# A graph layer on one core: bins ordered by branch, norms and input sums as queued VectorE steps, fillers between bin groups, first norms ahead of small loads

## The chip, the cores and the metric

The kernel runs on one core of a Trainium2 chip. TensorE (PE in the profile) multiplies matrices, VectorE (DVE) and ScalarE (ACT) work element by element, GpSimd (POOL) does a few small steps and issues some DMAs, SyncE (SP) issues most DMAs. Each engine works through its own list of instructions in order; semaphores join the lists. The metric is the device time of one execution in microseconds.

## The reference

64 graphs of 256 nodes with 256 features. All of it is float32.

```python
h = relu(layernorm(x))
# convolution branch: 1x1, then 17 taps along the nodes
c = relu(bn1(conv1(h)))
x_conv = relu(bn2(conv2(c)) + h)
# message branch
s = h @ w_se.T + b_se                       # 3 columns
A = exp(-|s_n - s_m|^2) * adj
x_nmp = A @ relu(h @ w_msg.T + b_msg)
# GRU gates
gi = [x_conv, x_nmp] @ w_ih.T + b_ih;  gh = h @ w_hh.T + b_hh
r = sigmoid(gi_r + gh_r); z = sigmoid(gi_z + gh_z)
n = tanh(gi_n + r * gh_n)
out = x + (1 - z) * n + z * h
```

## The kernel before

Graphs go in tiles of two (`G = 2`), so there are 32 tiles `i`; four tiles (`PB`) make a block `b`, and there are eight blocks. The convolution of 17 taps is done as a transform of length 16 along the nodes: products of the transformed input with the transformed filter in 16 bins, two bins at a time, so eight calls `products(b, 0)` to `products(b, 7)`, called P0 to P7 in the prediction. Bins 0 to 7 (P0 to P3) are the odd bins, the others the even bins. Each call uses three of five PSUM buffers "acc"; ScalarE copies one, VectorE subtracts and adds (lines 639, 640) into `Yv` (odd) or `Yu` (even, the same memory as V). There are three other PSUM buffers, "aux", for all else.

The forward transform is made by `fft.odd` (on V, with the sums in `Sv`) and `fft.even` (on U, with `PT`), the inverse by `odd_back`, `q_back`, `p_back` and `join`; `residual` then applies bn2 and a relu and gives the gates their operand `Yv`. T is scratch for all of these.

Before the first block a prologue makes the transformed filters: 57 calls of `filters` (one or two matmuls of 256 columns of `points` with `taps`, a copy by ScalarE into one of six buffers `fo`, a store to DRAM on SyncE's queue). They are read back bin by bin as `wb` (three buffers, SyncE's queue). In the prologue also run, for each of the first four tiles, `transpose_h` (transposes on TensorE, relu on ScalarE into `hT`, and the load of the x of two tiles later), `norm` of the next tile, `conv1`, and `split` (line 560: sums and differences of conv1's output `h1` into V and U).

In a block, tiles i to i+3 get their messages and gates while the next four tiles get norm, transposes, conv1 and split. `embed` makes s on TensorE and four small ScalarE steps (lines 664 to 667) on a single pair of tiles `ld`, `rd`; `message` a matmul, an add of the bias on VectorE (line 680) and a relu; `affinity` the exponent on ScalarE and the product with adj on VectorE (line 695); `transpose_a` and `aggregate` follow. `gates` needs twelve matmul passes with `Yv` (rows `acc<-Yv,w_ih`) after the rest.

The order of TensorE's work is written out by hand in the loop over blocks. The order on VectorE comes from a planner, `Pace`: it adds up the assumed time of TensorE and VectorE; steps of the transforms wait in one queue, and as many of them are put ahead of a direct VectorE instruction as fit before its operand is due. `flush(mark)` empties the queue up to a mark. Norm and split are direct instructions before the change. HW DMAs of SyncE and ScalarE use eight semaphores in turn, and an issue waits for the DMA that had its semaphore before.

Of the kernel before, what the change touches and what calls it, by code (L numbers as in the profile page):

```python
# [41 lines left out]
class Fft:  # L42
# [97 lines left out]

    def odd_back(self, Y, T):
# [5 lines left out]
        for h, t in ((0, T16), (2, T5)):  # L147
            q += [self.stt(Y(1, h, 2), T(1, h, 2), t, T(0, h, 2)),
                  self.stt(Y(1, h + 4, 2), T(0, h, 2), -t, T(1, h, 2))]
        even, odd = (lambda c, s: Y(c, s, 2, 2)), (lambda c, s: Y(c, s + 1, 2, 2))  # L150

        q += [self.sub(T(0, 0, 4), Y(0, 0, 4, 2), Y(0, 1, 4, 2)),
              self.sub(T(1, 0, 2), even(1, 0), odd(1, 4)),
              self.add(T(1, 2, 2), even(1, 4), odd(1, 0)),
              self.add(Y(0, 0, 4, 2), Y(0, 0, 4, 2), Y(0, 1, 4, 2)),
              self.add(even(1, 0), even(1, 0), odd(1, 4)),
              self.sub(even(1, 4), even(1, 4), odd(1, 0))]
        for h in (0, 2):
            q += [self.stt(Y(None, h + 1), T(None, 2 + h // 2), T8, T(None, h // 2)),
                  self.stt(Y(None, h + 5), T(None, h // 2), -T8, T(None, 2 + h // 2))]  # L160
# [106 lines left out]
ROOTS = [cmath.exp(1j * math.pi * (f + 16 * c) / 16) for c in (0, 1) for f in (1, 9, 5, 13)]  # L267
# [25 lines left out]
def kernel(  # L293
# [75 lines left out]
    def load_x(i):  # L369
        X[i] = work.tile([P, G * MC, D], FP, name="x", bufs=2)  # L370
        load_rows(X[i], x, i, nc.sync)

    def load_adj(i):
        ADJ[i] = work.tile([P, G * MC, N], FP, name="adj")
        load_rows(ADJ[i], adj, i, nc.gpsimd)
# [20 lines left out]
    def vec(src, name):  # L396
        k = src.shape[0] // P
        t = const.tile([P, k], FP, name=name)
        nc.sync.dma_start(out=t, in_=src.rearrange("(k p) -> p k", p=P))
        return t  # L400

    def fold_bn(params, name, factor=1.0):
        g, b, m, v = (vec(a, f"{name}_{s}") for a, s in zip(params, "gbmv"))
# [10 lines left out]


# [10 lines left out]
    w_c1 = const.tile([P, DC, D], FP)  # L426
    nc.scalar.dma_start(out=w_c1, in_=c1_wT.rearrange("(k p) o -> p k o", p=P))
    s1, h1_shift = fold_bn(bn1, "bn1")
# [15 lines left out]
    w_se = const.tile([P, DC, KD], FP)  # L444
    nc.gpsimd.memset(w_se, 0.0)
    for r in (0, 32, 64):
        nc.gpsimd.dma_start(out=w_se[:, :, r:r + SE], in_=se_wT.rearrange("(k p) s -> p k s", p=P))
    b_se = const.tile([P, 1], FP)
    for r in (0, 32, 64):
        nc.gpsimd.dma_start(out=b_se[r:r + SE, :], in_=se_b.rearrange("(s o) -> s o", o=1))  # L450
    w_msg = const.tile([P, DC, D], FP)
    nc.sync.dma_start(out=w_msg, in_=msg_wT.rearrange("(k p) o -> p k o", p=P))
    b_msg = const.tile([P, D], FP)
    nc.gpsimd.dma_start(out=b_msg, in_=bass.AP(tensor=msg_b.tensor, offset=msg_b.offset, ap=[[0, P], [1, D]]))
    load_adj(0)

    w_ih = const.tile([P, 2 * DC, 3 * D], FP)
    w_hh = const.tile([P, DC, 3 * D], FP)
    s2, h2_shift = fold_bn(bn2, "bn2", 1.0 / L)
    b_ih, b_hh = vec(ih_b, "b_ih"), vec(hh_b, "b_hh")  # L460
    b_rz = const.tile([P, 2 * DC], FP)
    nc.vector.tensor_add(b_rz, b_ih[:, :2 * DC], b_hh[:, :2 * DC])
    nc.vector.tensor_scalar(b_rz, b_rz, 0.5, None, ALU.mult)
    b_se2 = const.tile([P, 1], FP)
    nc.vector.tensor_scalar(b_se2[0:SE, :], b_se[0:SE, :], 2.0, None, ALU.mult)

# [21 lines left out]
    pace = Pace()  # L488

    def mm(p, w, v, columns, **kw):  # L490
        nc.tensor.matmul(p, w, v, **kw)  # L491
        pace.tensor(columns)

    def transpose(p, v):
        nc.tensor.transpose(p, v, ident)  # L495
        pace.tensor(P / 2)

    PSUM, ACT = 0.2, 0.9

    HT, MSG, E, AT, XNM = {}, {}, {}, {}, {}  # L500


    def norm(i):
        if i >= B // G:
            return
        st = work.tile([P, G * MC, 6], FP, name="st")
        mv = work.tile([P, G * MC, 2], FP, name="mv")
        for j in range(G * MC):
            pace.vector(D)
            nc.vector.bn_stats(st[:, j, :], X[i][:, j, :])  # L510
        for j in range(G * MC):
            pace.vector(1)
            nc.vector.bn_aggr(mv[:, j, :], st[:, j, :])
        rstd = work.tile([P, G * MC], FP, name="rstd")
        pace.vector(1)
        nc.vector.tensor_scalar(rstd, mv[:, :, 1], LN_EPS, None, ALU.add)
        nc.gpsimd.tensor_tensor(rstd, rstd, neg_half, ALU.pow)
        pace.vector(0, pace.dve + 1.4)
# [418 lines left out]
```

## Time and profile before

| | us |
|---|---|
| runs (three) | 2120.24, 2119.30, 2120.24; median 2120.24 |
| profiled execution, its own time | 2119.11 |
| its span | 2117.3 |
| TensorE busy | 1944.6 (92%) |
| VectorE busy | 1396.6 (66%) |
| ScalarE busy | 648.0 (31%) |
| GpSimd busy | 162.8 (8%) |
| first P0 begins | 143.01 |
| granted TensorE clock, mean | 0.977 |

A row of the timeline gives start, duration, engine, line, operation, tiles (out<-in), shape, how many followed each other, and in brackets the idle time of the engine before and what ended it. TensorE does each float32 matmul in two passes, so its counts are twice those of the program; durations of its groups include the end of the last pass, so starts are subtracted rather than ends. PEld is its weight load, SPq and ACTq are DMA issues on the queues of SyncE and ScalarE. In a list of waits the three numbers are the total, the count and the longest.

### The profile page before, as it was taken

The page shows a single profiled execution, that of the slowest core. Times are in us where ns is not written, and L with a number is a line of the kernel's source. Part 1 is how long each engine was busy: PE and PEld are TensorE (multiplying, and loading weights), DVE is VectorE, ACT ScalarE, POOL GpSimd, SP SyncE. Part 2 cuts the span into 40 slices and gives each one's busy share as a digit, 9 for nine tenths or more (in the row PEclk, how much of TensorE's full clock was granted, in tenths as well). Part 3 has the DMA queues.
Part 4 walks back from the last instruction along what each step waited for, and adds up shares of the span by engine and source line. Part 5 has one row for each costly group of instructions (what it writes and reads, how often), then busy time and mean ns, then how long its engine had stood idle before and what let it go on. Part 6 is the DMA issues. An engine that isn't in the chain of part 4 may idle for free.

```text
span 2117.3 us, 21204 instructions
## 1 busy us (share of the span) xinstructions
PE 1944.6 (92%) x7966; PEld 1221.2 (58%) x7966; DVE 1396.6 (66%) x2580; ACT 648.0 (31%) x1050; POOL 162.8 (8%) x246
## 2 busy tenths in 40 slices
PE   0889899998999899998999989998999989999897
PEld 0669445774449544694456844586455944568453
DVE  1379846796387845968367873879549784688532
ACT  0543422243313432224322432224322243223221
POOL 2000010100000001000001001000010100100000
PEclk9999999999999999999999999999999999999999
DMA  4766011540116202170124501163021711135010
GB/s 130 245 186 201 20 31 54 159 140 10 50 55 200 80 20 75 50 229 20 40 55 128 163 18 40 55 189 100 17 67 34 230 46 35 40 99 153 8 34 26
DMA packets 94164, 187.12 MB, mean 88 GB/s; under 512 B 23118, under 2 KB 40014, under 8 KB 94062
## 3 DMA queue, kind: packets, MB, share of 16 engines
q1 hardware_dynamic: 63368, 132.58, 20.1%
q0 software_dynamic: 27888, 50.58, 9.0%
q10 hardware_dynamic: 2806, 2.61, 0.4%
q8 instruction: 62, 1.02, 0.2%
q14 instruction: 40, 0.33, 0.0%
HBM read 156.55 MB, written 29.10 MB: 88 GB/s over the span
## 4 chain that ended last, share of the span: by engine, by line
PE 76%; DVE 13%; DMA 5%; ACT 3%; issue 2%; SPq 1%; POOL 1%; ACTq 0%; POOLq 0%; DVEq 0%
PE acc L491 58%; PE aux L491 15%; PE aux L495 3%; DMA wb<-filt 3%; DVE V L61 2%; DVE Yv L64 1%; DVE T L64 1%; DVE Yv L656 1%; DVE V L64 1%; DVE T L61 1%; DVE V L58 1%; DMA taps<-in_c_wT_dram 1%; DVE e L695 1%; SPq L442 1%; ACT Yv L657 1%
## 5 line engine op out<-in xcount | busy, mean ns | idle before, releaser
L491 PE MATMUL acc<-Yv,w_ih 128*128 128x512 f32 x768 | 359.1, 619 | 46.8 <-ACT Yv L657 46.8
L491 PE MATMUL acc<-hT,w_hh 128*128 128x512 f32 x768 | 350.6, 592 | 0.0
L491 PE MATMUL acc<-xnm,w_ih 128*128 128x512 f32 x768 | 350.4, 592 | 0.0
L491 PEld LDWEIGHTS acc<-Yv,w_ih 128*128 128x128 f32 x768 | 152.2, 199 | 244.7 <-issue 187.1
L491 PEld LDWEIGHTS acc<-xnm,w_ih 128*128 128x128 f32 x768 | 145.9, 190 | 183.7 <-issue 183.7
L491 PEld LDWEIGHTS acc<-hT,w_hh 128*128 128x128 f32 x768 | 144.1, 190 | 161.6 <-issue 156.7
L744 ACT ACTIVATE tr<-acc,b_rz 128x512 f32<-128x512 f32 x64 | 44.0, 687 | 553.7 <-PE acc L491 553.7
L746 DVE SCALAR_TENSOR_TENSOR gn<-tr,gn 128x512 f32<-128x512 f32 x64 | 44.2, 691 | 210.5 <-ACT tr L744 210.5
L560 DVE TENSOR_TENSOR V<-h 128x512 f32<-128x512 f32 x64 | 44.0, 688 | 157.7 <-ACT h L546 157.7
L491 PE MATMUL aux<-w_msg,hT 128*128 128x256 f32 x512 | 116.5, 380 | 12.9 <-ACT rd L667 12.9
L491 PE MATMUL acc<-V,wb 128*128 128x128 f32 x1024 | 126.1, 277 | 0.0
L491 PE MATMUL aux<-aT,msg 128*128 128x256 f32 x512 | 124.8, 400 | 0.6 <-ACT aT L706 0.6
L491 PEld LDWEIGHTS acc<-U,wb 128*128 128x128 f32 x1024 | 120.0, 192 | 5.1 <-issue 2.5
L491 PE MATMUL acc<-U,wb 128*128 128x128 f32 x1024 | 122.1, 275 | 0.0
L491 PEld LDWEIGHTS acc<-V,wb 128*128 128x128 f32 x1024 | 121.0, 194 | 0.0
L58 DVE SCALAR_TENSOR_TENSOR V<-T,V 128x256 f32<-128x256 f32 (+2 forms) x224 | 120.0, 609 | 0.3
L491 PE MATMUL acc<-hT,w_c 128*128 128x512 f32 x256 | 117.3, 601 | 1.1 <-ACT hT L533 1.1
L491 PEld LDWEIGHTS aux<-w_msg,hT 128*128 128x128 f32 x512 | 96.1, 190 | 35.2 <-ACT rd L667 14.6
L491 PEld LDWEIGHTS aux<-aT,msg 128*128 128x128 f32 x512 | 101.2, 202 | 19.3 <-issue 3.8
L495 PE MATMUL aux<-ident,x 128*128 128x128 f32 x256 | 37.1, 285 | 72.8 <-DVE x L521 51.6
L491 PE MATMUL acc<-Sv,wb 128*128 128x128 f32 x512 | 70.2, 281 | 21.5 <-DMA wb<-filt 13.9
L772 POOL DMA_DIRECT2D out_dram<-y x64 | 39.1, 615 | 642.3 <-DVE y L771 618.8
(124 smaller groups left out, 2662.8 us busy)
## 6 DMA issues: line engine op xcount, KB each, us to landing
wb<-filt SPq DMA_DIRECT2D x120, 768.0 KB
x<-in_x_dram SPq DMA_DIRECT2D x64, 256.0 KB
adj<-in_adj_dram POOLq DMA_DIRECT2D x64, 256.0 KB, 5.7
y<-in_x_dram POOLq DMA_DIRECT2D x64, 256.0 KB, 4.2
out_dram<-y POOLq DMA_DIRECT2D x64, 256.0 KB, 5.1
filt<-fo SPq DMA_DIRECT2D x36, 252.0 KB
wb<-filt SPq DMA_DIRECT2D x8, 512.0 KB
filt<-fo SPq DMA_DIRECT2D x18, 154.0 KB
```

What stands on the lines that cost most here:

```text
L58: return self.step(out, lambda: self.v.scalar_tensor_tensor(out, x, s, y, op0=ALU.mult, op1=ALU.add))
L61: return self.step(out, lambda: self.v.tensor_add(out, x, y))
L64: return self.step(out, lambda: self.v.tensor_sub(out, x, y))
L442: nc.sync.dma_start(out=taps[dc * REST * TAPS:(dc + 1) * REST * TAPS, DC * NG, :], in_=c2_wT[dc * P + NG * KG:(dc + 1) * P].rearrange("k t ...
L491: nc.tensor.matmul(p, w, v, **kw)
L495: nc.tensor.transpose(p, v, ident)
L560: nc.vector.tensor_sub(V(None, s, 4)[:, A], a, bb)
L656: nc.vector.scalar_tensor_tensor(v, v, s2[:, o:o + 1], HT[i][:, o, :], op0=ALU.mult, op1=ALU.add)
L657: nc.scalar.activation(v, v, AF.Relu, bias=h2_shift[:, o:o + 1])
L744: nc.scalar.activation(tr, pr, AF.Tanh, bias=b_rz[:, dc:dc + 1], scale=0.5)
L746: nc.vector.scalar_tensor_tensor(gn, tr, 1.0, gn, op0=ALU.add, op1=ALU.mult)
L772: nc.gpsimd.dma_start(out=rows(out, G * i + g), in_=row_tile(Y[i], g))
```

## The change

1. The odd bins are numbered so that P0 and P1 hold one branch of the inverse transform (h = 0) and P2 and P3 the other. `odd_back` loses its first two levels to `branch_back`, which is queued once per branch: the first after P1, the second after P3. They are cut into smaller steps.
2. `norm` is cut into `norm_steps` (statistics, and scaling) and `split` into `split_steps`; in the block these go into the planner's queue, with marks `normed` and `halved`.
3. Message, embed, affinity, transposes, finish and aggregate are spread in another order between the products, and the order in the gates part changes: `transpose_a(i + 2)` before the second gates, `message(i + 3)` before `embed(i + 3)`, and `aggregate(i + 2)` before the transposes of `nxt + 1`.
4. In the prologue norm 0 and norm 1 come first, bn1 is loaded on ScalarE's queue, all taps on SyncE's in three chunks per half, x 2 and x 3 on ScalarE's queue, adj 0 on SyncE's, bn2 and the gate biases on GpSimd's; bn2 is folded after the odd transform; the filter calls go half by half (`steps`), four per tile instead of twelve; w_hh and w_ih are loaded on ScalarE's queue after the last filter.

```diff
+    def branch_back(self, Y, T, h):
+        t = T5 if h else T16
...
+        q = [self.sub(d(0, 0, 2), Y(0, h, 2), Y(1, h, 2)),
...
     def odd_back(self, Y, T):
-
         q = []
-        for s in (0, 4):
-            q += [self.sub(T(s // 4, 0, 4), Y(0, s, 4), Y(1, s, 4))]
-        q += [self.add(Y(0, 0, 8), Y(0, 0, 8), Y(1, 0, 8))]
...
-ROOTS = [cmath.exp(1j * math.pi * (f + 16 * c) / 16) for c in (0, 1) for f in (1, 9, 5, 13)]
+ROOTS = [cmath.exp(1j * math.pi * (f + 8 * h + 16 * c) / 16) for f in (1, 5) for c in (0, 1) for h in (0, 1)]
...
     for dc in range(DC):
-        for h in range(2):
-            load_taps(dc, h * NG // 2, (h + 1) * NG // 2, nc.scalar if dc else nc.sync)
+        for h in range(3):
+            load_taps(dc, h * NG // 3, (h + 1) * NG // 3, nc.sync)
...
         if i + 2 < B // G:
-            load_x(i + 2)
+            load_x(i + 2, nc.scalar if i < 2 else nc.sync)
...
-            c, h = n // 4, n % 4
+            c, h = n // 2 % 2, n // 4 * 2 + n % 2
...
-    steps = [(m, j) for m in range(len(PASSES)) for j in range(NG + 1)]
-    norm(0)
+    steps = [(m, j) for m, dc in ((0, 0), (1, 0), (0, 1), (2, 0), (1, 1), (2, 1)) for j in chunks[dc]]
+    transpose_h(0)
+    norm(1)
...
+    load_y(0)
+    load_y(1)
+    pace.flush(odd)
+    s2, h2_shift = fold_bn(bn2, "bn2", 1.0 / L)
...
         embed(i)
-        message(i)
         pace.flush(odd)
         products(b, 0)
+        message(i)
+        products(b, 1)
+        pace.add(fft.branch_back(Yv, T, 0))
         affinity(i)
+        embed(i + 1)
+        products(b, 2)
+        transpose_a(i)
         if b > 0:
             finish(i - 1)
-        products(b, 1)
-        transpose_a(i)
-        products(b, 2)
-        aggregate(i)
         products(b, 3)
         pace.flush(even)
+        pace.add(fft.branch_back(Yv, T, 2))
         pace.add(fft.odd_back(Yv, T))
-        embed(i + 1)
+        aggregate(i)
         products(b, 4)
...
+        stats, scale = norm_steps(nxt + 1)
+        join(0)
+        pace.add(stats)
+        join(1)
+        pace.add(scale, normed)
+        pace.add(split_steps(nxt), halved)
+        join(2)
+        join(3)
...
         gates(i, 0, wait)
+        transpose_a(i + 2)
+        gates(i, 1)
+        aggregate(i + 2)
+        pace.flush(normed)
+        transpose_h(nxt + 1)
+        pace.flush(halved)
+        conv1(nxt + 1)
...
         gates(i + 1, 0)
+        message(i + 3)
         embed(i + 3)
+        pace.flush(normed)
         transpose_h(nxt + 2)
-        message(i + 3)
         conv1(nxt + 2)
```

The first place is the start of VectorE's list, before: the fold of bn1 (not shown), that of bn2 and the biases of the gates and of s stand ahead of the first norm, which begins with `BN_STATS`.

```order
L406 TENSOR_SCALAR bn_scale<-bn_v 128x2
L408 TENSOR_TENSOR bn_scale<-bn_scale,bn_g 128x2
L409 TENSOR_TENSOR bn_shift<-bn_m,bn_scale 128x2
L410 TENSOR_TENSOR bn_shift<-bn_b,bn_shift 128x2
L412 TENSOR_SCALAR bn_scale<-bn_scale 128x2
L462 TENSOR_TENSOR b_rz<-b_ih,b_hh 128x4
L463 TENSOR_SCALAR b_rz<-b_rz 128x4
L465 TENSOR_SCALAR b_se_160<-b_se 3x1
L510 BN_STATS st<-x 128x6 x4
```

The same place after the change:

```order
L427 BN_STATS st<-x 128x6 x4
L431 BN_AGGR mv<-st 128x2 x4
L432 TENSOR_SCALAR rstd<-mv 128x4
L436 TENSOR_SCALAR x<-x,mv,rstd 128x256 x4
L469 TENSOR_SCALAR bn_scale<-bn_v 128x2
L471 TENSOR_TENSOR bn_scale<-bn_scale,bn_g 128x2
L472 TENSOR_TENSOR bn_shift<-bn_m,bn_scale 128x2
L473 TENSOR_TENSOR bn_shift<-bn_b,bn_shift 128x2
```

Norm 0 is VectorE's first work now, then the fold of bn1, then norm 1.

The second place is VectorE around P0 of the first block, before: Sv ends the odd transform, PT begins the even one; the first two rows to Yv take P0's result.

```order
L61 TENSOR_TENSOR Sv<-V 128x2048
L61 TENSOR_TENSOR PT<-U 128x2048
L64 TENSOR_TENSOR U<-U 128x32x64
L61 TENSOR_TENSOR T<-PT 128x32x32
L639 TENSOR_TENSOR Yv<-p_806,acc 128x16x32
L640 TENSOR_TENSOR Yv<-p_806,acc 128x16x32
```

And after (L643 and L644 are the lines that were 639 and 640, L684 adds the message's bias; L469 to L475 fold bn2, with the power on POOL between L469 and L471):

```order
L61 TENSOR_TENSOR Sv<-V 128x2048
L469 TENSOR_SCALAR bn_scale<-bn_v 128x2
L471 TENSOR_TENSOR bn_scale<-bn_scale,bn_g 128x2
L472 TENSOR_TENSOR bn_shift<-bn_m,bn_scale 128x2
L473 TENSOR_TENSOR bn_shift<-bn_b,bn_shift 128x2
L475 TENSOR_SCALAR bn_scale<-bn_scale 128x2
L843 TENSOR_TENSOR b_rz<-b_ih,b_hh 128x4
L844 TENSOR_SCALAR b_rz<-b_rz 128x4
L846 TENSOR_SCALAR b_se_751<-b_se 3x1
L61 TENSOR_TENSOR PT<-U 128x2048
```

and, after seven more steps of the even transform, to P0's result and the first message add:

```order
L58 SCALAR_TENSOR_TENSOR U<-T,U 128x32x16 x4
L64 TENSOR_TENSOR T<-PT 128x16x16
L61 TENSOR_TENSOR T<-PT 128x16x16
L58 SCALAR_TENSOR_TENSOR T<-U 128x16x32 x2
L58 SCALAR_TENSOR_TENSOR PT<-T,PT 128x16x16 x4
L58 SCALAR_TENSOR_TENSOR U<-T,U 128x16x16
L643 TENSOR_TENSOR Yv<-p_791,acc 128x16x32
L644 TENSOR_TENSOR Yv<-p_791,acc 128x16x32
L58 SCALAR_TENSOR_TENSOR U<-T,U 128x16x16
L684 TENSOR_TENSOR msg<-aux,b_msg 128x256 x2
```

Between Sv and P0's result stood three instructions of the even transform; now there are the fold of bn2, the biases and 21 instructions of it.

The third place is VectorE from P2's to P3's result in the second block, before: the pairs to Yv stand next to each other, and the inverse transform of the odd bins begins only then.

```order
L639 TENSOR_TENSOR Yv<-p_2189,acc 128x16x32
L640 TENSOR_TENSOR Yv<-p_2189,acc 128x16x32
L639 TENSOR_TENSOR Yv<-p_2239,acc 128x16x32
L640 TENSOR_TENSOR Yv<-p_2239,acc 128x16x32
L64 TENSOR_TENSOR T<-Yv 128x16x64 x2
L61 TENSOR_TENSOR Yv<-Yv 128x16x128
L58 SCALAR_TENSOR_TENSOR Yv<-T 128x16x32 x4
```

After:

```order
L643 TENSOR_TENSOR Yv<-p_2180,acc 128x16x32
L644 TENSOR_TENSOR Yv<-p_2180,acc 128x16x32
L775 TENSOR_TENSOR y<-aux,y 128x512 x2
L58 SCALAR_TENSOR_TENSOR Yv<-T 128x16x32
L64 TENSOR_TENSOR T<-Yv 128x16x32
L64 TENSOR_TENSOR T<-Yv 128x16x16
L61 TENSOR_TENSOR T<-Yv 128x16x16
L61 TENSOR_TENSOR Yv<-Yv 128x16x2x16
L61 TENSOR_TENSOR Yv<-Yv 128x16x16
L64 TENSOR_TENSOR Yv<-Yv 128x16x16
L643 TENSOR_TENSOR Yv<-p_2251,acc 128x16x32
L644 TENSOR_TENSOR Yv<-p_2251,acc 128x16x32
```

The steps of the first branch now stand between the results of P2 and P3 (five of them even ahead of P2's).

More of the change, by code (lines that the diff above doesn't have):

```diff
@@ L486, in acc @@
         return psum.tile([P, W], FP, name="acc", bufs=5)
[L488 to L518, printed above, removed]
-        for j in range(G * MC):
-            pace.vector(D)
-            nc.vector.tensor_scalar(X[i][:, j, :], X[i][:, j, :], mv[:, j, 0:1], rstd[:, j:j + 1],
-                                    ALU.subtract, ALU.mult)
     def transpose_h(i):
@@ L784, in mix @@
         return q
-    odd, even, q_done = Mark(), Mark(), Mark()
+    odd, even, normed, halved = (Mark() for _ in range(4))
     joined = [Mark() for _ in range(PB)]
@@ L856 @@
         gates(i, 0, wait)
-        pace.flush(joined[1])
-        split(nxt)
-        norm(nxt + 1)
-        gates(i, 1)
-        transpose_a(i + 2)
-        transpose_h(nxt + 1)
-        aggregate(i + 2)
-        conv1(nxt + 1)
-        pace.flush(joined[3])
-        split(nxt + 1)
-        norm(nxt + 2)
+        transpose_a(i + 2)
[5 more added lines that the diff above has]
+        conv1(nxt + 1)
+        stats, scale = norm_steps(nxt + 2)
+        pace.add(stats)
+        pace.add(split_steps(nxt + 1), halved)
+        pace.add(scale, normed)
+        pace.flush(joined[1])
         gates(i + 1, 0)
+        message(i + 3)
         embed(i + 3)
+        pace.flush(normed)
         transpose_h(nxt + 2)
-        message(i + 3)
         conv1(nxt + 2)
-        split(nxt + 2)
+        stats, scale = norm_steps(nxt + 3)
+        pace.add(stats)
+        pace.add(split_steps(nxt + 2), halved)
+        pace.add(scale, normed)
         finish(i)
-        norm(nxt + 3)
         gates(i + 1, 1)
@@ L878 @@
         gates(i + 2, 0)
+        pace.flush(normed)
         transpose_h(nxt + 3)
@@ L881 @@
         conv1(nxt + 3)
-        split(nxt + 3)
+        pace.add(split_steps(nxt + 3), halved)
         if b + 1 < NB:
```

172 lines of the change are left out of this document (110 added, 62 removed).

## The prediction

> **What bounds the kernel now.** I read the waits of TensorE first (who ended them, total, count, longest), since TensorE is busy for 92% of the span and only its gaps can be won.
>
> ```profile
> PE aux L495 <- DVE x L521: 51.6, 1, 51.6
> PE acc L491 <- ACT Yv L657: 46.8, 8, 5.9
> PE aux L495 <- ACT aT L706: 21.2, 7, 3.0
> PE acc L491 <- DMA wb<-filt: 13.9, 7, 2.8
> PE aux L491 <- ACT rd L667: 12.9, 7, 1.9
> ```
>
> So there is one long wait at the start, and four that come back in each of the eight blocks. The timeline of one block (start, duration, engine, what, idle before) shows them in place; a block starts where its first bin product P0 starts.
>
> ```profile
> 639.09 1.05 PE L491 MATMUL acc<-Sv,wb 128*128 128x128 f32 x8
> 658.10 1.16 PE L491 MATMUL acc<-Sv,wb 128*128 128x128 f32 x8 [1.96 <-DMA wb<-filt]
> 660.88 3.62 PE L491 MATMUL aux<-aT,msg 128*128 128x256 f32 x16
> 729.04 7.42 PE L491 MATMUL acc<-Yv,w_ih 128*128 128x512 f32 x12 [5.88 <-ACT Yv L657]
> 746.60 5.31 PE L491 MATMUL acc<-Yv,w_ih 128*128 128x512 f32 x12
> 756.26 0.66 PE L495 MATMUL aux<-ident,x 128*128 128x128 f32 x4 [3.04 <-ACT aT L706]
> 756.76 5.41 PE L491 MATMUL aux<-aT,msg 128*128 128x256 f32 x16
> 785.49 3.72 PE L491 MATMUL aux<-w_msg,hT 128*128 128x256 f32 x16 [1.85 <-ACT rd L667]
> 882.96 1.88 PE L491 MATMUL aux<-hT,w_se 128*67 128x512 f32 x4
> 884.68 3.62 PE L491 MATMUL aux<-w_msg,hT 128*128 128x256 f32 x16
> 888.13 1.05 PE L491 MATMUL acc<-Sv,wb 128*128 128x128 f32 x8
> 907.13 2.05 PE L491 MATMUL acc<-Sv,wb 128*128 128x128 f32 x8 [1.96 <-DMA wb<-filt]
> ```
>
> A block lasts 888.13 - 639.09 = 249.0 us. Waits are followed by slow matmuls: the same twelve take 7.42 us after the wait and 5.31 without (2.1 lost), the same sixteen 5.41 against 3.62 (1.8 lost). The block loses 5.88 + 2.1, 3.04 + 1.8, 1.96, and 1.85 + 0.1: 16.7 us.
>
> The longest of the four is VectorE's doing. After P3's result it works almost without a pause up to the residual that frees the gates; just before, it sits idle.
>
> ```profile
> 661.15 0.69 DVE L639 TENSOR_TENSOR Yv<-p,acc 128x512 f32<-128x512 f32 x1 [5.52 <-PE acc L491]
> 669.96 0.69 DVE L639 TENSOR_TENSOR Yv<-p,acc 128x512 f32<-128x512 f32 x1 [7.53 <-PE acc L491]
> 671.16 2.35 DVE L64 TENSOR_TENSOR T<-Yv 128x1024 f32<-128x1024 f32 x2
> 673.55 2.29 DVE L61 TENSOR_TENSOR Yv<-Yv 128x2048 f32<-128x2048 f32 x1
> 675.88 2.50 DVE L58 SCALAR_TENSOR_TENSOR Yv<-T 128x512 f32<-128x512 f32 x4
> 727.42 1.42 DVE L656 SCALAR_TENSOR_TENSOR Yv<-Yv,bn_scale,hT 128x512 f32<-128x512 f32 x2
> ```
>
> **Part 1, bins by branch.** The inverse transform of the odd bins had to wait for P3. Its first two levels are 14 to 15 us (7.1 in the three groups shown, about as much again in the level behind them); half of them now needs P0 and P1 alone and fits the idle 5.52 + 7.53 us, beside the message adds (1.5) that also come in there. Finer steps cost 0.5 us more. From P3's end VectorE needed 727.42 + 1.42 - 669.8 = 59.0 us; now 59.0 - 7.3 + 0.3 + a last relu of 0.7 = 52.7. TensorE reached the wait after 729.04 - 5.88 - 669.8 = 53.4 us; the new order puts an aggregate (3.45) behind P3 and takes an embed (1.72) from there: 55.1. The wait goes, with 2.4 us to spare, and its 2.1 of slow clock.
>
> **Part 2, the other waits of a block.** The transposed affinity gets a whole gates stage of cover, so 3.04 + 1.8 go. The message no longer stands behind the embedding's four ScalarE steps (1.85 + 0.1), but the next thing behind them is now conv1: the order is message, embed, transposes, conv1, and hT comes after the four steps on ScalarE.
>
> ```profile
> 782.60 1.04 PE L495 MATMUL aux<-ident,x 128*128 128x128 f32 x8
> 785.46 1.08 ACT L533 ACTIVATE hT<-aux 128x512 f32<-128x512 f32 x2
> ```
>
> The first hT is ready at about 786.1; the transposes end 0.87 after 782.60. conv1 would wait **2.6 us** where the message waited 1.85: this wait is new. Bounds: 1.9 (the old wait) to 4.4 (all of it cold). A second conv1 now follows its transposes with no aggregate between: 0.6 us. Clock: a wait of 1.96 cost nothing at 658 and 0.9 on the first group at 907, about 1.7 with the next; 3.04 cost 1.8. I take 0.7 on average for the 2.6.
> The Trainium skill (TensorE: Matmul & The Clock Gate, Part 1) says that the clock falls after an idle window of about 3.4 us. By that, 2.6 us would cost no clock and the total would be 5 us lower; the row at 907.13 speaks against it, and the measurement decides.
> The filter load's 1.96 us fell between P1 and P2, with one 0.9 us filler between them; now 3.45 us stands there, while P2 to P3 has 1.7 instead of 3.45. Bounds 0 to 2; I take 0.3, as the total of loads is unchanged and no group pair is now as tight as the old one while stores run.
> Queued steps (stats, scale, split) cost what they did and stand beside gates matmuls: covered. **Block: -16.7 + 2.6 + 0.6 + 0.7 + 0.3 = -12.5.** Six blocks (P0 to P0): **-75**. The last one has no conv1: -2.0 (load), -8.0 (gates wait and clock), +1.0 for a rest of the gates wait (no conv1 stands before it to give cover), and +3.45 since its message is now behind P0: **-5.5**.
>
> **Part 3, the front.**
>
> ```profile
> 8.08 0.37 SPq L399 DMA_DIRECT2D bn_m<-in_bn_m_dram  x1
> 9.96 12.07 SPq L423 DMA_DIRECT2D taps<-in_c_wT_dram  x2
> 45.79 0.17 DVE L406 TENSOR_SCALAR bn_scale<-bn_v 128x2 f32<-128x2 f32 x1 [28.37 <-DMA bn_v<-in_bn_v_dram]
> 47.93 1.40 DVE L510 BATCH_NORM_STATS2 st<-x 128x6 f32<-128x256 f32 x4
> 51.58 2.30 PE L495 MATMUL aux<-ident,x 128*128 128x128 f32 x8 [51.58 <-DVE x L521]
> 59.00 10.53 PE L491 MATMUL acc<-taps,points 119*126 119x256 f32 x48
> 69.36 1.04 PE L495 MATMUL aux<-ident,x 128*128 128x128 f32 x8
> 74.28 10.10 PE L491 MATMUL acc<-taps,points 119*126 119x256 f32 x46
> 143.01 2.05 PE L491 MATMUL acc<-Sv,wb 128*128 128x128 f32 x8 [7.58 <-issue]
> taps<-in_c_wT_dram SPq DMA_DIRECT2D x2, 1071.0 KB
> 32.00:36.00 4.00, 0.00 (x0) 0.00 (x0) 0.00 (x0) 0.00 (x0) 0.00 (x0) 1.00 0.47 169
> ```
>
> VectorE's first norm stood behind small loads that landed at 45.79. x is there by 8.08: SyncE held that issue until the second half of x 0 had landed. So TensorE can start at 8.1 + (51.58 - 47.93) = 11.8, against 51.58. It won't keep the whole 40 us. The tap loads (4 x 1071 KB) are all on SyncE now, ahead of w_msg, adj and every store of a filter. At 169 GB/s (the window's last number) from 10 us on they end at 36 to 37; with w_msg and adj the first store lands at about 43. Bounds: 38 and 55. There are six store buffers, so ScalarE blocks at the seventh copy, and behind it the third hT. By 43 TensorE has done two conv1 and eight filter steps; left are 49 steps of 0.88 (10.53 / 12), two conv1 with transposes (74.28 - 69.36 = 4.9 each) and an embed of 1.7: 43.1 + 9.8 + 1.7 = 54.6, with 2 of cold clock: P0 at about **100**, against 143.0 (**-43**). If TensorE were the only bound, P0 would come at about 88 (11.8, 57 x 0.88, 4 x 4.9, 1.7 and 4 of cold clock); if the stores start at 55, at 112.
> On "Issuing engines are not separate DMA queues" (DMA: Bandwidth & Descriptors) the Trainium skill says that loads issued by different engines run on the same 16 DMA engines, so moving ScalarE's half of the taps to SyncE would cost nothing and 43 stands; a quarter slower on one queue would make P0 8 us later. No row here shows one queue alone.
>
> **Part 4, a new stall in block 0.** The second bn fold now stands on VectorE between Sv and the even transform, and needs a POOL power that is queued behind the four y loads; these wait for the last filter matmul, since y takes the place of the taps.
>
> ```profile
> 16.11 0.72 POOL L407 TENSOR_TENSOR bn_scale<-bn_scale,neg_half 128x2 f32<-128x2 f32 x1 [14.74 <-DVE bn_scale L406]
> 22.77 0.61 POOL L367 DMA_DIRECT2D adj<-in_adj_dram  x1 [0.28 <-DMA w_se<-in_se_wT_dram]
> 637.57 0.76 DVE L680 TENSOR_TENSOR msg<-aux,b_msg 128x256 f32<-128x256 f32 x2
> 643.04 1.43 DVE L58 SCALAR_TENSOR_TENSOR PT<-T,PT 128x256 f32<-128x256 f32 x4
> ```
>
> Four issues of 0.61 and 0.72 put the power at P0 + 1.5 (the last filter is an embed before P0); eight small steps: P0 + 3.5. Then come, by the order, 21 steps of the even transform (by the rows of Part 1 and these 2.2 per 2048 elements, 1.1 per 1024, 0.6 per 512, 0.34 per 256): 15.1 us, so that P0's own subtract runs at P0 + 18.6 and the first message add ends at P0 + 20.9. TensorE: P0 5.4, message 3.5, P1 5.4 and half an affinity, then at P0 + 15.1 it needs the message's PSUM buffer (three "aux"). Stall 5.8, another 0.6 for the embed, 1.4 for the affinity's transposes (their multiply ends at 30.9): 7.8, with 1.7 of cold clock and 1.0 for w_ih and w_hh, which now load here beside the filters: **+10.5** (bounds 0 and 15). Of the old losses 14.7 go (no filter wait here) and the slow start of P0 (2.05 against 1.05 in its first group): 15.7; 3.9 of the new waits of Part 2 come: -15.7 + 10.5 + 3.9 = **-1.3**.
>
> **Sum.** -43 - 1.3 - 75 - 5.5 = -124.8 on a span of 2117.3: 1992.5. The profiled run took 2119.1, 1.8 more than its span and 1.1 less than the median of 2120.2, so I expect 1992.5 + 2.9, or **1995** (-5.9%).
>
> **Rivals.**
> 1. *The store queue holds the front longer*: tap chunks run one after the other, stores start at 55, P0 at 112: 1995 + 12 = 2007. For it: SyncE's issue of taps took 12.07 us in the row at 9.96. 0.10.
> 2. *The waits move on*: VectorE is 6 us later at the residual than worked out (margin 2.4, so 3.6 + 2.1 lost), the filter wait stays (1.7 more), the conv1 wait is always cold (1.1 more): 8.5 a block less won, 4 left. 1995 + 60 = 2055 over seven blocks; half of it, 2025. For it: VectorE has no pause between 670 and 729. Against: the steps that go are counted in its rows. 0.12.
> 3. *Slower*: block 0's stall comes in every block. If VectorE enters each block so late that P0's subtract runs 18.6 us behind P0, TensorE waits 9.5 there, and the gates wait returns with 7 + 2.4: 19 a block over seven blocks, 133: 2128. It decides from a lag of about 9 us at P0's end, where the message's buffer is late. In later blocks no POOL step stands between Sv and the even transform, and laying the rows behind 882.96 in the new order gives a subtract at 8.8 us after that row's gates, P0 ending at 7.1. 0.03.
> 4. *Front and block 0 without stalls*: P0 at 90, VectorE's 21 even steps done earlier: 1995 - 20 = 1975. 0.08.
>
> My forecast has 0.67. The range 1970 to 2027 takes in the bounds of the front (-12, +12), of block 0 (-10, +5), of the filter wait (+12) and of the clock, and half of rival 2; about 0.8. Only differences over 0.2% can be told from no change here: faster 0.95, the same 0.02, slower 0.03.
>
> **What would show it.** TensorE's first matmul near 12 and P0 near 100; a stop of some 10 us before that on a filter's copy; in block 0 a wait on the message add of about 6 us; no wait on the Yv relu in blocks 1 to 6; a conv1 wait on hT of 2.6 us seven times; P0 to P0 at 236 to 237 us. A gates wait of over 2 us, or a block over 241, proves Part 1 or 2 wrong; P0 outside 90 to 110 proves Part 3 wrong.

## The result, and the profile after

The changed kernel took 1999.76 us (median of 4 runs, 1997.96 to 2002.96) against 2120.24 for the kernel before (4 runs): a ratio of 0.9427, 95% interval 0.9404 to 0.9451. The forecast was 1995. The profiled execution has a span of 1999.7 us, 117.6 less than before.

TensorE's largest waits in the changed kernel (who ended them; total, count, longest):

```profile
PE acc L404 <- ACT hT L537: 33.4, 16, 13.7
PE aux L408 <- DVE x L436: 10.7, 1, 10.7
PE acc L404 <- DMA wb<-filt: 10.1, 2, 8.6
```

The rows of the Yv relu, of aT and of rd are gone, and the filter load has two waits where it had seven. The wait on hT has grown: it was 1.1 us in all before. The timeline of one steady block (start, duration, engine, what, idle before) shows the places of the old waits:

```profile
596.15 1.05 PE L404 MATMUL acc<-Sv,wb 128*128 128x128 f32 x8
...
681.31 5.31 PE L404 MATMUL acc<-Yv,w_ih 128*128 128x512 f32 x12
...
707.57 3.70 PE L404 MATMUL acc<-hT,w_c 128*128 128x512 f32 x8 [0.30 <-ACT hT L537]
...
735.24 5.32 PE L404 MATMUL acc<-hT,w_c 128*128 128x512 f32 x8 [2.47 <-ACT hT L537]
...
832.59 1.05 PE L404 MATMUL acc<-Sv,wb 128*128 128x128 f32 x8
```

Two waits are left in a block, both of conv1 on hT: 0.30 and 2.47 us. The block lasts 236.44 us; six of them, from the second P0 at 361.34 to the last at 1774.83, average 235.58 (before: 249.1).

| stretch of the span | before | after | difference | forecast |
|---|---|---|---|---|
| start to first P0 | 143.01 | 113.48 | -29.5 | -43 |
| block 0 | 247.05 | 247.86 | +0.8 | -1.3 |
| blocks 1 to 6 | 1494.55 | 1413.49 | -81.1 | -75 |
| last block to the end | 232.7 | 224.9 | -7.8 | -5.5 |
| sum | 2117.3 | 1999.7 | -117.6 | -124.8 |

The front gave 13.5 us less than forecast and block 0 2.1 less; blocks 1 to 6 gave 6.1 more and the last 2.3 more. So the total is right partly by luck: misses on both sides nearly cancel. The front, TensorE first, then ScalarE:

```profile
10.70 2.30 PE L408 MATMUL aux<-ident,x 128*128 128x128 f32 x8 [10.70 <-DVE x L436]
57.77 6.13 PE L404 MATMUL acc<-hT,w_c 128*128 128x512 f32 x8 [13.67 <-ACT hT L537]
72.11 30.39 PE L404 MATMUL acc<-taps,points 119*126 119x256 f32 x140
...
55.92 1.30 ACT L581 COPY fo<-acc 126x512 f32<-126x512 f32 x2 [13.11 <-DMA filt<-fo]
```

The stop has the forecast place: ScalarE stands at its seventh filter copy for a store to land, behind it the third hT, behind that conv1. But the first store landed at 55.9, not 43. In block 0 a filter load stops TensorE, not the message add that the forecast named; VectorE's rows stand behind TensorE's:

```profile
131.01 2.04 PE L404 MATMUL acc<-Sv,wb 128*128 128x128 f32 x8 [8.56 <-DMA wb<-filt]
152.15 1.16 PE L404 MATMUL acc<-Sv,wb 128*128 128x128 f32 x8 [1.58 <-DMA wb<-filt]
...
131.45 0.68 DVE L643 TENSOR_TENSOR Yv<-p,acc 128x512 f32<-128x512 f32 x1
132.98 0.75 DVE L684 TENSOR_TENSOR msg<-aux,b_msg 128x256 f32<-128x256 f32 x2
```

VectorE is as late as forecast (P0's subtract at P0 + 18.0, forecast 18.6), but TensorE was already waiting for a load until 131.01.

### The profile page after: what moved, and what is told of

The parts are those of the page before. It is cut to its first block, busy times and chain, and to the rows that moved or that the text cites. A ratio compares the mean times of both kernels' runs of the same rounds, so it can differ in the third digit from the quotient of the medians.

```text
span 1999.7 us, 21268 instructions
## 1 busy us (share of the span) xinstructions
PE 1922.1 (96%) x7966; PEld 1210.7 (61%) x7966; DVE 1401.8 (70%) x2668; ACT 642.2 (32%) x1050; POOL 170.1 (9%) x250
## 4 chain that ended last, share of the span: by engine, by line
PE 92%; DMA 4%; ACT 2%; SPq 1%; issue 1%; POOL 0%; ACTq 0%; DVE 0%; POOLq 0%; DVEq 0%
PE acc L404 72%; PE aux L404 16%; PE aux L408 3%; DMA wb<-filt 1%; DMA taps<-in_c_wT_dram 1%; DMA filt<-fo 1%; SPq L489 1%; ACT hT L537 0%; SPq L505 0%; DMA bn_m<-in_bn_m_dram 0%; ACT ld L670 0%; ACT rd L671 0%; ACT ld L668 0%; ACT xnm L720 0%; ACT rd L669 0%
## 5 line engine op out<-in xcount | busy, mean ns | idle before, releaser
L404 PE MATMUL acc<-Yv,w_ih 128*128 128x512 f32 x768 | 340.0, 592 | 0.0
L404 PEld LDWEIGHTS acc<-Yv,w_ih 128*128 128x128 f32 x768 | 145.9, 190 | 183.7 <-issue 181.5
L404 PE MATMUL acc<-hT,w_c 128*128 128x512 f32 x256 | 127.1, 643 | 33.4 <-ACT hT L537 33.4
L404 PE MATMUL aux<-aT,msg 128*128 128x256 f32 x512 | 115.8, 379 | 0.0
L404 PEld LDWEIGHTS aux<-aT,msg 128*128 128x128 f32 x512 | 96.1, 190 | 19.2 <-issue 5.7
L775 DVE TENSOR_TENSOR y<-aux,y 128x512 f32<-128x512 f32 x64 | 41.1, 684 | 93.0 <-PE aux L408 93.0
L404 PEld LDWEIGHTS acc<-hT,w_c 128*128 128x128 f32 x256 | 50.7, 207 | 90.2 <-ACT hT L537 44.0
L372 POOL DMA_DIRECT2D adj<-in_adj_dram x62 | 37.2, 604 | 629.7 <-DVE e L699 605.3
```

What stands on the lines that cost most here:

```text
L372: eng.dma_start(out=row_tile(t, g), in_=rows(src, G * i + g))
L775: nc.vector.tensor_add(row_tile(Y[i], g), p, row_tile(Y[i], g))
```

## The experiments

All start from the changed kernel. A time with an interval is from several rounds; the others are one run each (the kernel before took 2124.36 beside e4 to e7, 2121.73, a median of 7, beside e8, and 2121.81, a median of 9, beside e11) and are read by their traces. Where P0 begins in each run, by the timelines (us):

| run | time | first P0 | block 0 | mean of blocks 1 to 6 |
|---|---|---|---|---|
| changed kernel | 1999.76 | 113.48 | 247.9 | 235.58 |
| e1 | 2054.69 | 114.56 | 251.5 | 242.38 |
| e2 | 2001.65 | 112.87 | 250.2 | 235.63 |
| e3 | 1976.69 | 114.75 | 241.2 | 232.46 |
| e4 | 1990.19 | 107.40 | 242.4 | 235.62 |
| e5 | 1993.35 | 102.82 | 250.0 | 235.65 |
| e6 | 1999.16 | 109.46 | 249.1 | 235.65 |
| e7 | 1994.57 | 111.47 | 242.8 | 235.61 |
| e8 | 2002.17 | 118.08 | 244.2 | 235.51 |
| e9 | 2003.04 | 111.88 | 250.0 | 235.41 |
| e10 | 1961.13 | 106.07 | 234.6 | 232.56 |
| e11 | 1965.22 | 104.29 | 239.1 | 232.50 |
| e12 | 2077.28 | 111.80 | 256.8 | 245.77 |

Block 0 varies by 8 us between kernels that do not touch it (e2, e4 to e7, e9), so there only waits are read, not its length. The front varies too: six kernels have the same one (the changed kernel, e1, e2, e3, e9, e12), and in them P0 begins between 111.80 and 114.75 and the first store lands between 53.3 and 55.9. A shift inside these ranges can't be told from none; the changed kernel itself lies near their late end.

### The front: e4 to e7

**e4**, half of the tap loads back on ScalarE's queue:

```diff
-            load_taps(dc, h * NG // 3, (h + 1) * NG // 3, nc.sync)
+            load_taps(dc, h * NG // 3, (h + 1) * NG // 3, nc.scalar if dc else nc.sync)
```

> The changed kernel with the second half of the tap loads put back on ScalarE's queue; all else as in the changed kernel. There ScalarE stood at the seventh filter copy until 55.92 us, conv1 of the third tile started at 57.77 and P0 at 113.48. Theory A (one queue carries the taps more slowly than two: about 107 GB/s here against 169 before the change): taps and so the first filter store end some 8 us earlier, conv1 of the third tile starts at 48 to 51, P0 at 103 to 107. Theory B (the queues share the same transfer engines, and the taps are slow because the small loads and the x loads now run beside them): no change, P0 at 112 to 115.

**e5**, eight store buffers:

```diff
-        t = stage.tile([P, 2, D], FP, name="fo", bufs=6)
+        t = stage.tile([P, 2, D], FP, name="fo", bufs=8)
```

> The changed kernel with eight store buffers (fo) instead of six, which is as many as fit. Theory A (ScalarE stands at the seventh copy for want of a buffer, and the third hT behind it): the copies 7 and 8 pass, the third hT and conv1 of the third tile run at about 45 instead of 57.8, the stop moves to the first filter of the third tile, and P0 comes some 5 to 6 us earlier, at 107 to 109. Theory B (the buffers only hide the order of the DMA queue; what counts is when the last stores go out): P0 at 112 to 114.

**e6**, the small loads later (the lines from `w_se = const.tile` to `b_ih, b_hh = vec(...)`, without w_msg and adj, moved from ahead of the `for j in range(PB)` loop to behind it):

> The changed kernel with the GpSimd loads of w_se, b_se, b_msg, the four vectors of the second batch norm, b_ih and b_hh issued behind the last norm of the first block (about 60 us) instead of at 20 to 40 us. Theory B (the taps are slowed by these small loads beside them: 107 GB/s from 20 to 40 us, 167 GB/s at 45 to 50 when the taps are alone): first filter store some 6 to 8 us earlier, conv1 of the third tile at 49 to 52, P0 at 104 to 108. Theory A (one queue is the limit): P0 within 1.5 us of 113.5.

**e7**, the two larger loads moved in the same way:

```diff
     for j in range(PB):
...
             filters(m, n)
+    w_msg = const.tile([P, DC, D], FP)
+    nc.sync.dma_start(out=w_msg, in_=msg_wT.rearrange("(k p) o -> p k o", p=P))
+    load_adj(0, nc.sync)
     forward()
```

> The changed kernel with the loads of w_msg and adj 0 (768 KB, on SyncE's queue between the taps and the first filter store) issued behind the first sixteen filters instead. Theory (the first store waits its turn behind them): the first store is issued 4 to 5 us earlier, conv1 of the third tile at 53 to 54, P0 at 109 to 110. Rival (the store waits for the taps' landing alone, on a DMA lane or behind their bytes): P0 within 1 us of 113.5.

What all DMA moved from 26 to 34 us, while the small loads run beside the taps (the last number is GB/s, the one before it the busy share of the 16 DMA engines), in the changed kernel:

```profile
26.00:34.00 8.00, 6.51 (x18) 4.36 (x19) 2.93 (x11) 1.78 (x3) 2.96 (x4) 0.63 0.55 129
```

with the taps on two queues (e4):

```profile
26.00:34.00 8.00, 8.00 (x18) 4.05 (x17) 0.00 (x0) 0.00 (x0) 0.81 (x1) 1.00 0.61 171
```

with one queue, but without the small loads beside it (e6):

```profile
26.00:34.00 8.00, 8.00 (x24) 5.02 (x24) 1.38 (x4) 1.78 (x3) 1.01 (x1) 0.74 0.48 162
```

and in the changed kernel just behind, when the taps run alone on SyncE's queue:

```profile
34.00:38.00 4.00, 3.79 (x15) 2.44 (x13) 0.00 (x0) 0.00 (x0) 0.00 (x0) 1.00 0.48 165
```

Alone, one queue moves what two moved before the change: 165 GB/s here, 169 in the window that the prediction shows, with the same share of the engines busy. Beside the small loads it does not: the nine kernels with one queue and the small loads there move 129 to 148 from 26 to 34 us, the three with one queue and without them (e6, e10, e11) 158 to 163, e4 171. So both theories hold in part: the small loads slow the taps when one queue carries them, and in e4, a single run, two queues made up for it. (The 107 GB/s of the expectations stands in no row: from 20 to 40 us SyncE's queue moved 2.43 MB in the changed kernel, 121 GB/s.)

In e4 the stop at the seventh copy is gone, though ScalarE, held at its own tap issues, made its first hT only at 24.80 and conv1 waited 12.37 us for it; P0 came 6.1 us earlier, just short of the forecast, and 4.4 earlier than in any kernel with the untouched front. In e6 the first store lands at 52.50 and P0 comes 4.0 earlier, but only 2.3 earlier than the earliest untouched front: less than theory B wanted, and its size is not shown. The Trainium skill (DMA: Bandwidth & Descriptors, Issuing engines are not separate DMA queues) says that a second issuing engine saves issue time only, as all queues run on the same 16 engines. The 165 of one queue alone against 169 of two agrees; the 171 against 129 to 148 with the small loads beside does not, and there the measurement decides. That two queues get a larger share than one against a third would fit, but was not tried by itself.

In e5 conv1 of the third tile starts at 42.27 instead of 57.77, and the stop moves one tile on:

```profile
57.99 5.44 PE L404 MATMUL acc<-hT,w_c 128*128 128x512 f32 x8 [6.41 <-ACT hT L537]
```

P0 is 10.7 us earlier (9.0 earlier than any untouched front), where 5 to 6 were expected: the first two tiles make eight copies, so with eight buffers the whole third tile passes, its filter matmuls included. In e7 the third tile's conv1 starts at 51.94, 5.8 us earlier, but the filters then wait 0.87 and 2.71 us for their copies, where the changed kernel has 1.58. The moved loads now run among the stores. P0 comes 2.0 earlier where 4 were expected, and at 111.47 hardly outside the range of the untouched fronts, so no gain of P0 is shown.

### Block 0: e8

w_hh and w_ih on GpSimd's queue behind the first block's norms:

```diff
+    nc.gpsimd.dma_start(out=w_hh, in_=hh_wT.rearrange("(k p) o -> p k o", p=P))
+    nc.gpsimd.dma_start(out=w_ih, in_=ih_wT.rearrange("(k p) o -> p k o", p=P))
     forward()
...
-    nc.scalar.dma_start(out=w_hh, in_=hh_wT.rearrange("(k p) o -> p k o", p=P))
-    nc.scalar.dma_start(out=w_ih, in_=ih_wT.rearrange("(k p) o -> p k o", p=P))
```

> The changed kernel with w_hh and w_ih (2.36 MB) issued by GpSimd behind the last norm of the first block, at about 60 us, instead of by ScalarE at 112 us. In the changed kernel block 0 (P0 to P0 of block 1) takes 247.9 us, 12 more than the blocks behind it, and waits 8.6 and 1.6 us for filter loads. Theory C (the filter loads wait for bytes of w_hh, w_ih and y; under that wait lies the later message add that the prediction named, since VectorE does its even steps only behind the second fold): the filter wait falls under 1.5 us, and a wait of 5 to 6 us at the affinity (its PSUM buffer, held by the message add) and one of 1 to 2 us at its transposes appear: block 0 at 242 to 246. Rival D (the message add was never a bound): the filter wait goes and nothing takes its place, block 0 at 235 to 238. Rival E (the filter loads wait for their place in SyncE's queue, not for bytes): the filter wait stays above 6 us, block 0 at 246 to 249. The front may lose up to 4 us, since these loads then run beside the filter stores.

```profile
130.12 1.13 PE L404 MATMUL acc<-Sv,wb 128*128 128x128 f32 x8 [3.07 <-DMA wb<-filt]
138.35 2.01 PE L404 MATMUL aux<-rd,ld 67*128 67x256 f32 x4 [1.77 <-DVE msg L684]
140.15 3.62 PE L404 MATMUL aux<-hT,w_se 128*67 128x512 f32 x4
```

The filter wait falls from 8.56 to 3.07, and the message add appears behind it, ahead of the affinity's second half, whose buffer it holds, with the slow clock behind it (the embed takes 3.62 where it takes 1.88 in the changed kernel). Theory C's mechanism, split otherwise: 3.07 + 1.77 instead of under 1.5 and 5 to 6; the wait at the transposes does not come. P0 is 4.6 us later (3.3 later than in any untouched front), so nothing is won. Rival E falls: it asked for more than 6 us. That bytes are what the load waits for agrees with the changed kernel, where SyncE issued it at 114.83, 16 us before P1 could start, and the DMA engines are full from P0 to the end of that wait (0.99):

```profile
112.00:131.00 19.00, 10.45 (x68) 8.70 (x67) 15.53 (x27) 3.78 (x7) 3.19 (x5) 0.91 0.99 295
```

A later filter load, at 123.24, was held at its issue, 6.5 us of it until w_hh landed; so for the second wait of 1.58 us the place may count too.

### The steady blocks: e1, e2, e9, e12, e3

**e1**, Part 1 undone: the old `odd_back`, `ROOTS`, `operands` and places in Yv, and no `branch_back`:

```diff
-        pace.add(fft.branch_back(Yv, T, 0))
...
-        pace.add(fft.branch_back(Yv, T, 2))
         pace.add(fft.odd_back(Yv, T))
```

> The changed kernel with the old numbering of the odd bins and the old inverse of all of them behind P3; everything else as in the changed kernel. Theory (the gates wait went because half of the first two inverse levels runs before P3): about 6.7 us of VectorE steps come back behind P3, where the changed kernel has 0.6 us to spare (last relu ends at 680.7, the gates' Yv matmuls start at 681.31) and up to 1.9 us of idle VectorE: a gates wait of 4 to 6 us and about 2 us of slow clock in each block, P0 to P0 at 242 to 244 instead of 235.6, and 2045 to 2060 us in all. Rival (the gates wait went because norms and input sums left VectorE's path there, the bins' order adds little): wait under 1 us, P0 to P0 within 1 us, 1998 to 2008.

```profile
PE acc L399 <- ACT Yv L656: 31.9, 8, 4.0
```

The ratio to before is 0.968 (0.9666 to 0.9695). The gates wait is back, 4.0 us in each of eight blocks, and with its slow clock a block is 6.8 us longer: the theory holds.

**e2**, the transposed affinity in its old place:

```diff
-        transpose_a(i + 2)
         gates(i, 1)
-        aggregate(i + 2)
+        transpose_a(i + 2)
         pace.flush(normed)
         transpose_h(nxt + 1)
+        aggregate(i + 2)
```

> The changed kernel with the transposed affinity of the third group put back behind the second gates stage, directly ahead of the next transposes, and the aggregate behind them. Theory (the whole gates stage of cover is what took the wait on aT away): a wait of 3.0 us on aT's copy with about 1.8 us of slow clock comes back in each of seven or eight blocks, partly offset by 0.3 us that the following conv1 no longer waits: P0 to P0 at 239.5 to 240.5, 2028 to 2036 us in all. Rival (the wait went with the norms and splits in front of it, the place does not matter): under 0.5 us a block, 1997 to 2004.

0.9428 (0.9412 to 0.9444): no difference. The theory falls: of 3.04 us of wait 0.83 are back, without slow clock, and conv1's 0.30 goes. That leaves 0.5 us, and it is hidden by the clock: conv1's wait of 2.47 us is followed by slow matmuls in two of seven blocks here, in four in the changed kernel. With the new bins the cover of a gates stage was hardly needed. **e9** asks whether norms and input sums ahead of the gates steps had made the old wait: e2 with

```diff
+        pace.flush(halved)
         gates(i, 1)
         transpose_a(i + 2)
```

> The kernel of e2 (transposed affinity back in its old place) in which, besides, VectorE runs the queued steps up to the input sums of group nxt ahead of the second gates stage, as before the change, instead of spreading them beside it. e2 alone had a wait on aT of 0.83 us, where the kernel before had 3.04, and P0 to P0 at 235.6. Theory F (the old wait came from norms and input sums in front of the gates steps: they delayed VectorE, with it ScalarE's tanh, and the copy of aT queued behind that): the wait on aT comes back at 2 to 3 us with 1 to 1.8 us of slow clock, P0 to P0 at 238.5 to 240.5, 2018 to 2032 us. Rival G (the old wait was an echo of the gates wait that is gone): the wait stays under 1.2 us, P0 to P0 within 0.7 us of 235.6, 1998 to 2006.

0.9437 (0.9424 to 0.945): the wait stays at 0.83, so these steps alone do not make it either. **e12** is e9 with the old bins of e1 besides:

> The kernel of e9 (transposed affinity in its old place, queued steps run out ahead of the second gates stage) with the old order of the bins besides, so that the gates wait of e1 (4.0 us a block) is there too. In e9 the wait on aT stayed at 0.83 us. Rival G of e9 (the old wait of 3.04 us was an echo of the gates wait: TensorE then follows right behind VectorE, whose remaining joins reach into the second gates stage, delay its tanh and with it the copy of aT): the wait on aT comes back at 2 to 3.2 us with 1 to 1.8 us of slow clock, P0 to P0 at 245 to 247.5 where e1 has 242.4, 2070 to 2090 us in all. If the wait stays under 1.2 us here too (P0 to P0 at 242 to 243.5, 2050 to 2062), the gates wait is not its cause either, and what took it away stays open.

0.9793 (0.9777 to 0.981). Now the wait is back:

```profile
PE acc L399 <- ACT Yv L656: 31.8, 8, 4.0
PE aux L403 <- ACT aT L705: 20.9, 7, 3.0
```

The rows of one block of e12, VectorE, ScalarE, TensorE:

```profile
716.81 1.38 DVE L431 TENSOR_SCALAR x<-x,mv,rstd 128x256 f32<-128x256 f32 x4
718.10 0.69 DVE L64 TENSOR_TENSOR V<-h 128x512 f32<-128x512 f32 x1
...
727.14 1.41 DVE L655 SCALAR_TENSOR_TENSOR Yv<-Yv,bn_scale,hT 128x512 f32<-128x512 f32 x2
728.47 0.68 DVE L745 SCALAR_TENSOR_TENSOR gn<-tr,gn 128x512 f32<-128x512 f32 x1
...
724.17 0.69 ACT L743 ACTIVATE tr<-acc,b_rz 128x512 f32<-128x512 f32 x1 [5.95 <-PE acc L399]
731.19 1.06 ACT L705 COPY aT<-aux 128x512 f32<-128x512 f32 x2
...
731.81 0.66 PE L403 MATMUL aux<-ident,x 128*128 128x128 f32 x4 [3.00 <-ACT aT L705]
```

and the same of e9:

```profile
702.02 0.68 DVE L750 SCALAR_TENSOR_TENSOR gn<-tr,gn 128x512 f32<-128x512 f32 x1
...
699.90 0.69 ACT L748 ACTIVATE tr<-acc,b_rz 128x512 f32<-128x512 f32 x1 [9.25 <-PE acc L404]
704.75 1.06 ACT L710 COPY aT<-aux 128x512 f32<-128x512 f32 x2
```

In e12 VectorE is still busy with the last joins and residuals when the gates' tr is ready at 724.86, and takes it up at 728.47, 3.6 us later; in e9 it is 1.4 later (702.02 against 700.59). The copy of aT stands behind that step's tanh on ScalarE: 7.02 us after tr's start against 4.85. The difference of 2.17 is the 3.00 against 0.83. So the wait on aT was in part an echo of the gates wait: with TensorE waiting for VectorE there, everything that VectorE still owes reaches into the next stage. Between e9 and e12 lies Part 1 alone, and it is worth 10.4 us a block (245.77 - 235.41), 74 us in all.

But the gates wait is not enough. Ahead of those joins VectorE scales a norm and makes four input sums (716.81 to 720.5 in e12, 3.7 us), the steps that theory F named. e1 has the same gates wait of 4.0 us, with these steps later and the transposed affinity in its new place, and there VectorE takes tr up at once (718.61, ready at 718.53):

```profile
717.84 0.69 ACT L743 ACTIVATE tr<-acc,b_rz 128x512 f32<-128x512 f32 x1 [9.67 <-PE acc L399]
718.61 0.68 DVE L745 SCALAR_TENSOR_TENSOR gn<-tr,gn 128x512 f32<-128x512 f32 x1
```

TensorE has no wait on aT in e1, and its blocks are 3.4 us shorter than those of e12 (242.38 against 245.77). So the new bins take the wait away, all but 0.83 us (e9), and so does the rest of the new order without them (e1). Which of the two counts in e1, the new place or the later steps, was not tried.

**e3**, the embed behind the transposes:

```diff
-        embed(i + 3)
         pace.flush(normed)
         transpose_h(nxt + 2)
+        embed(i + 3)
         conv1(nxt + 2)
```

> The changed kernel with the embed of the fourth group moved from ahead of the transposes of group nxt+2 to behind them, ahead of conv1. Theory (conv1 waits 2.47 us because hT stands behind the embed's four ScalarE steps): the wait goes, hT needs about 0.9 us behind the last transpose and the embed's matmuls take 1.72: 2.47 us and on average 0.8 us of slow clock less in each of seven blocks, P0 to P0 at 232.0 to 233.0 and without the alternation of 234.8 and 236.4, 1976 to 1982 us in all. Rival (the wait moves on: the transposes now need a PSUM buffer that the message's add on VectorE still holds, or the norm's scale that runs there): a new wait of 1.5 to 2.5 us at the transposes, 1994 to 2001.

```profile
490.77 1.93 PE L404 MATMUL aux<-hT,w_se 128*67 128x512 f32 x4
492.54 3.60 PE L404 MATMUL acc<-hT,w_c 128*128 128x512 f32 x8
```

0.9315 (0.9301 to 0.9329). The conv1 behind the embed waits no longer and runs in 3.60 each time (the other keeps its 0.30); a block is 3.1 us shorter, and the rival's wait at the transposes does not come.

### Together: e10 and e11

e10 joins e3 and e5 with later small loads, w_msg and adj 0 (GpSimd's queue), and

```diff
         filters(m, n)
+        if j == 8:
+            nc.scalar.dma_start(out=w_hh, in_=hh_wT.rearrange("(k p) o -> p k o", p=P))
+            nc.scalar.dma_start(out=w_ih, in_=ih_wT.rearrange("(k p) o -> p k o", p=P))
         if j == 20:
...
+    s2, h2_shift = fold_bn(bn2, "bn2", 1.0 / L)
     stage_ctx.close()
```

in place of the old lines. e11 leaves the fold where it was.

> The changed kernel with the embed behind the transposes (e3), eight store buffers (e5), the small loads, w_msg and adj 0 behind the last norm of the first block on GpSimd's queue (e6, e7), w_hh and w_ih at the ninth filter of the tail on ScalarE's queue, and the second batch norm folded ahead of the y loads. If the gains add: P0 at 95 to 100 (102.8 with the buffers alone, 4 from the small loads, 2 from w_msg and adj, up to 5 back to the weights beside the stores), block 0 at 233 to 238, since neither a filter load nor the message add is waited for, blocks at 232.5, the last at 224.9: 1948 to 1960 us. If the loads only move the wait: the stores are slowed by w_hh and w_ih, P0 at 101 to 106, or the first filter load of P1 still waits 3 us behind the y loads, block 0 at 239 to 242: 1960 to 1968.

> The kernel of e10 with the second batch norm folded behind the y loads, as in the changed kernel. Theory (with the filter wait gone, the late even steps of VectorE show in full): in block 0 the affinity waits 5 to 6 us for its PSUM buffer, held by the message add, and its transposes 1 to 2 us more; with 1 to 2 us of slow clock block 0 is 7 to 10 us longer than in e10. Rival: under 2 us longer.

e10 takes 1961.13 us, 0.9237 (0.9225 to 0.925), the fastest of all. The gains do not add in the front, as its second expectation had it: w_hh and w_ih run among the stores, the filters wait for their copies, and TensorE needs 45.0 us (59.26 to 104.30) for what took 39.6 (72.11 to 111.71). Block 0 does fall to 234.6, e3's 3 us included. In e11 the fold's price shows:

```profile
119.93 1.03 PE L404 MATMUL aux<-rd,ld 67*128 67x256 f32 x4
124.50 2.07 PE L404 MATMUL aux<-rd,ld 67*128 67x256 f32 x4 [3.54 <-DVE msg L684]
126.36 3.44 PE L404 MATMUL aux<-hT,w_se 128*67 128x512 f32 x4
```

3.54 us of wait and about 2.6 of slow clock (2.07 for half an affinity, 3.44 for an embed of 1.88). Block 0 is 4.5 longer than in e10, which has 1.5 of other waits there: more than the rival, less than the 7 to 10 expected.

## Why the prediction was right, and where not

**Part 1** was right. The gates wait went in all blocks, and e1 brings it back. The margin came out at 0.6 us instead of 2.4 (the last relu ends at 680.7, the Yv matmuls start at 681.31). VectorE pauses for 3.4 us on that way (1.85 us the longest); before the change it paused for 2.7 there (0.98, 0.97 and 0.60 the longest), so "no pause between 670 and 729" was misread, and the pauses explain 0.7 of the 1.8; the rest stays open. It was credited with 5.88 + 2.1 us a block; it is worth 6.8 in the new order (e1 against the changed kernel) and 10.4 in the old one (e12 against e9).

**Part 2** had the right sum (-12.5 a block, measured -13.5; of its four waits "in each of the eight blocks" three come only seven times) with one reason that is only half shown. "The transposed affinity gets a whole gates stage of cover, so 3.04 + 1.8 go": they went, but with the new bins all but 0.83 go without the new place (e2), and with the old bins the rest of the change takes them (e1 against e12). So Part 1 and the new order each remove this wait, and the credit can be given to neither alone. The new conv1 wait was right (2.6 forecast, 2.47 measured, seven times), and so was its cause (e3). The second conv1 waits 0.30 instead of 0.6, the filter load 0 instead of 0.3, the clock costs 0.8 on average instead of 0.7. The last block has no rest of a gates wait where 1.0 was put down, and its old gates wait cost 8.6 with the clock instead of 8.0; about 1 us more of it is not accounted for.

**Part 3** failed in one step: "At 169 GB/s (the window's last number) from 10 us on they end at 36 to 37; with w_msg and adj the first store lands at about 43." That rate came from a window in which two queues carried taps and nothing ran beside them. Here one queue carried them beside others. From 10 to 40 us the changed kernel moved, in MB (the second number), on SyncE's, ScalarE's and GpSimd's queue:

```profile
q1 hardware_dynamic: 3424, 3.48, 39.5%
q10 hardware_dynamic: 576, 0.64, 8.3%
q0 software_dynamic: 432, 0.15, 5.7%
```

The taps got 116 GB/s of 143: besides the lower rate, the sum left out the x loads on ScalarE's queue (0.64 MB). The first store landed at 55.9, P0 came at 113.48: past the 90 to 110 that the prediction set itself, and near the times of its first rival (stores from 55, P0 at 112). e5 and e4 each win part of it back; for e6 this is probable only.

**Part 4** had the right size for the wrong reason, in the changed kernel: +10.5 of stall forecast, of which 8.56 + 1.58 us and some slow clock came from a filter load. Priced at 1.0, "w_ih and w_hh, which now load here beside the filters", was the step that failed. The stall on the message add exists (e8, e11); in the changed kernel it lay hidden under the load. Removing both is what brings block 0 to 234.6.

## What to carry to other kernels

When several engines take turns in waiting, a later wait can be the echo of an earlier one, and two changes can each remove it: undo them one at a time and together before crediting either. A transfer rate read from one window holds only for the same mix of queues and neighbours. Before a shift of a few microseconds is called a result, read the same row in kernels that do not touch the place. And before removing the wait that shows, look at whether another engine is late at the same place: its wait comes up next.

## What was not expected of the hardware

The wait of 2.47 us before conv1 is equal in all seven blocks of the changed kernel, yet its price is not:

```profile
263.91 5.40 PE L404 MATMUL acc<-hT,w_c 128*128 128x512 f32 x8 [2.47 <-ACT hT L537]
500.42 3.70 PE L404 MATMUL acc<-hT,w_c 128*128 128x512 f32 x8 [2.47 <-ACT hT L537]
```

Four times the eight matmuls run slowly (5.16 to 5.40 us), three times at full speed (3.70), in turn; blocks last 236.4 and 234.8 accordingly. The Trainium skill (TensorE: Matmul & The Clock Gate, Part 1) lets the clock fall after at least one idle window of about 3.4 us, by a free-running window. A gap of 2.47 us should never cost anything by that, and here it does: ten kernels of this case have this wait seven times each, and behind 35 of the 70 the matmuls run slowly (in all seven blocks of e1, in one of e9). The length of the window agrees, though: with the time divided into periods of 3.413 us, the gaps with slow matmuls start in one part of the period and the others in the rest, in each of the ten kernels, and few other lengths do that. So a gap shorter than the window seems to be enough, depending on where it falls in it; how short, these runs do not show.
